# Four graph layers on one core: layer 0 in pairs of seven block products, one tile for the buffers, the softmax division on ScalarE

## Chip, core and metric

One core of a Trainium2 chip runs the whole program. Its engines are TensorE (PE in the profile, with weight loads as PEld), VectorE (DVE), ScalarE (ACT) and GpSimd (POOL); SyncE (SP) issues most of the DMAs. The metric is device time in microseconds, as the median of several runs. One run is also taken with a profile; its own time is given beside its span.

## What is computed

The input x is 128 batches of 128 nodes with 512 features, all fp32. Four graph layers follow one another, each added to its input and normalised over the features:

```python
x = _layernorm(x + _L0_gnn_ref(x, adj, L0_gnn_weight, L0_gnn_bias), axis=-1)
x = _layernorm(x + _L1_gnn_ref(x, L1_gnn_W, L1_gnn_a, L1_gnn_beta, adj), axis=-1)
x = _layernorm(x + _L2_gnn_ref(x, adj, adj, L2_gnn_b), axis=-1)
x = _layernorm(x + _L3_gnn_ref(x, L3_gnn_w_qkv, ..., L3_gnn_ln_beta, adj), axis=-1)
```

The two places that the change concerns are layer 0 and the softmax of layer 3:

```python
# layer 0
y = jnp.einsum('nm,bmd->bnd', adj, x)
out = jnp.einsum('bnd,do->bno', y, weight) + bias
# layer 3, 8 heads of 64
attn = jnp.where(attn_mask[None, None] == 0, -jnp.inf, attn)
attn = jax.nn.softmax(attn, axis=-1)
o = jnp.einsum('bhnm,bhmd->bhnd', attn, v)...
o = o @ w_proj + b_proj
```

Layer 1 is an attention with scores from two vectors per node, layer 2 a maximum over a product with adj. The batches do not depend on each other.

## The kernel before

**Planner.** The kernel is written as chains of steps, one per batch or group of batches (`batch`, L1031, is the main one). Each step asks the class `Plan` (L79) for an engine with an estimate of its work and, if need be, for buffers. `Plan.run` (L172) always takes the step that can start first (ties by urgency, then by the rank of its batch) and issues its instructions at once. So the order on each engine is fixed when the program is built; on the chip each engine runs its list in order and waits by semaphores. Estimates, hand-over times (`HANDOFF`), slack factors (`SLACK`), the margin that PE steps are put back by (`MARGIN`), and the limits per kind of buffer (`CAPS`) decide the order.

**Buffers.** `BUFS` (L49) gives 8 PSUM banks ("ps") and, in SBUF, 21 buffers of 2 KB a partition ("t"), 15 of 4 KB ("q") and 7 of 1 KB ("u"), each a tile of its own. `POOL` tells which kind a use ("x", "yT", "v", "qk", ...) is served from. Ten early batches of x are guests, two by two, in "q" buffers (`GUESTS`, `ROOMS`).

**Groups.** Batches go in groups of four (the last two groups have two). A batch passes layers 0, 1 and 2 by itself or in a pair; the queries, keys and values of layer 3 are made for a group. Weighted values are computed together with the scores of a group six later (`APART`, `tiled`), and by themselves in the last groups.

**Seven block products.** A product of a stacked pair of batches with a 512x512 weight is split into 2x2 blocks, and seven block products with sums of blocks take the place of eight (`seven`, L755). GpSimd makes four differences of the left blocks (`differences`, L833); the weights' sums are made once (`sums`, L547). A block product in `pair_product` (L845) is two matmuls 256 wide. Three banks hold partial sums. Where a partial sum is wanted twice, ScalarE copies it to the output buffer (`kept`, L760) and PE goes on adding to the same bank after that copy; VectorE adds another bank to the copy (`added`, L773). Layer 1 (`layer1`), the queries, keys and values (`section`) and the projection (`projection`) are done so.

**Layer 0.** The first twelve batches (`DIRECT`) take a direct way. From batch 12 on, `mixed_rows` (L337) multiplies by adj (L341), transposes on VectorE in 32x32 squares, and sends the result through DRAM to get it turned (yT). Then PE does one product of four matmuls, 512 wide, with the weight (L1050, by `product`, L314); GpSimd has meanwhile added the bias to x (L307); VectorE adds the product to x with the row sums (L1059), and `layernorm_sums` (L289) normalises, its squares going to the same PSUM bank, which nobody reads.

**Softmax of layer 3.** VectorE adds the mask and takes the negative maximum; ScalarE does one exp per head with the row sums (L1172); VectorE takes reciprocals and multiplies all heads by them in one instruction (L1179), then transposes (L1183). The last two batches (`WHOLE`) do the subtraction, one exp and the sums over all heads at once (L1162 to L1168). After the spill of x to DRAM (all but the last `KEPT` batches) and the fetch back, `normed` (L1291) ends the batch.

Of the kernel before, what the change touches and what calls it, by code (L numbers as in the profile page):

```python
# [15 lines left out]
P = 128  # L16
D = 512
# [5 lines left out]
SOON = (0, 0, 4, 8, 12, 16)  # L23
WHOLE = 2
KEPT = 5
ATTENDS = 2
RUN = 6
# [4 lines left out]
ROOMS = ["v"] * 4 + ["xT"] * 2 + ["qk"] * 5  # L32
STICK = 0.8
CLOSE = 2900
SOFT = 10
PROJ = 0
# [12 lines left out]
BUFS = {"ps": 8, "t": 21, "q": 15, "u": 7}  # L49
POOL = {"x": "t", "xr": "t", "yT": "t", "v": "q", "qk": "q", "xT": "q"}  # L50
CAPS = {"x": 8, "xr": 2, "yT": 6, "v": 4, "qk": 8, "xT": 4}
LAST, AHEAD = 16, 4
DIRECT = 12
LATER = 2
# [8 lines left out]
BORDERS = 0.0  # L63
MARGIN = 0.6
# [14 lines left out]
class Plan:  # L79
# [9 lines left out]
    def __init__(self):  # L89
        self.free, self.requests = {}, []  # L90
        self.slots = {name: [0.0] * n for name, n in BUFS.items()}
        self.caps, self.held = {name: [0.0] * n for name, n in CAPS.items()}, {}
        self.now, self.kind = 0.0, ""
# [21 lines left out]

    def give(self, slot):
        name, i = slot
        self.slots[POOL.get(name, name)][i] = self.now
        if name in CAPS:
            self.caps[name][self.held.pop(slot)] = self.now  # L120
# [16 lines left out]
    def at(self, r):  # L137
        engine, _, take, _, order, _ = r["want"]
        spare = MARGIN if r["ready"] < CLOSE else 0.7
        early = min(spare, r["ready"] / 20) if engine == "PE" and order else 0.0  # L140
        t = max(r["ready"] + early, self.free.get(engine, 0.0))
        names = take()
        for name, i in self.pick(names):
            t = max(t, self.slots[POOL.get(name, name)][i])
        for name in set(names) & set(CAPS):
            t = max(t, sorted(self.caps[name])[names.count(name) - 1])
        return t

    def pick(self, names):

        picked, taken = [], set()
        for name in names:
            pool = POOL.get(name, name)
            free = self.slots[pool]
            i = min((i for i in range(len(free)) if (pool, i) not in taken), key=free.__getitem__)
            picked.append((name, i))
            taken.add((pool, i))
        return picked

    def claim(self, names):  # L160

        got = self.pick(names)
        for name, i in got:
            self.slots[POOL.get(name, name)][i] = float("inf")
            if name in CAPS:
                caps = self.caps[name]
                n = caps.index(min(caps))
                caps[n] = float("inf")
                self.held[name, i] = n
        return got  # L170

    def run(self):  # L172
        while self.requests:
            t, _, _, n = min(
                (self.at(r) + self.border(r["want"]), r["want"][4], r["rank"], n)
                for n, r in enumerate(self.requests)
            )
            assert t < float("inf"), "the chains wait for each other"
            r = self.requests.pop(n)
            t = self.at(r)  # L180
            engine, work, take, late, _, kind = r["want"]
            if engine == "PE":
                work += BORDERS * (kind != self.kind)
                self.kind = kind
            self.free[engine] = t + work
            self.now = r["ready"] = t + work + late
            got = self.claim(take())
            self.step(r, got[0] if len(got) == 1 else got)
# [9 lines left out]
def gnn_stack_kernel(  # L198
# [25 lines left out]

    plan = Plan()
    use, give, done = plan.use, plan.give, plan.done

    def buf(slot, *shape):
        name, i = slot
        return work.tile([P, *shape], F32, name="{}_{}".format(POOL.get(name, name), i))  # L230
# [53 lines left out]
    def row_sums():  # L284

        n = small.tile([P, 6], F32, name="sums", bufs=14)
        return [n[:, c : c + 1] for c in range(6)]

    def layernorm_sums(xb, total, unread):  # L289

        total, nm, squares, ve, rstd, nmr = total
        yield use("DVE", 0.07, follow=True)
        nc.vector.tensor_scalar(nm, total, -1.0 / D, None, op0=ALU.mult)  # L293
        yield use("ACT", 1.03)
        nc.scalar.activation(buf_or_bank(unread), xb, AF.Square, bias=nm, accum_out=squares)  # L295
        give(unread)
        nc.scalar.activation(ve, squares, AF.Identity, bias=eps, scale=1.0 / D)  # L297
        yield from root(ve, rstd)
        yield use("ACT", 1.03)
        nc.scalar.activation(nmr, nm, AF.Identity, scale=rstd)  # L300
        nc.scalar.activation(xb, xb, AF.Identity, bias=nmr, scale=rstd)  # L301
# [99 lines left out]
    wsum_sb = const.tile([P, 3 + SEVEN1 + SEVENP, 3, 2, D // 2], F32, name="wsum_sb")  # L401
# [12 lines left out]
    w0_chunk = [Event() for _ in range(K)]  # L414
    scalars_in, w0_in, w3_in, wa_ready, w3_ready = (Event() for _ in range(5))
# [8 lines left out]
    def load(i, engine="SP", queue=nc.sync):  # L424
        n = i - CAPS["x"]
        if 0 <= n < GUESTS:
            slot = yield use(engine, 0.5, () if n % 2 else ROOMS[n // 2])
            x_slot[i] = x_slot[i - 1] if n % 2 else slot
            if not n % 2:
                room[slot] = buf(slot, 2, D)  # L430
                guests[slot] = 2
            xs[i] = room[x_slot[i]][:, n % 2]
        else:
            x_slot[i] = yield use(engine, 0.5, "x")
            xs[i] = buf(x_slot[i], D)
        queue.dma_start(xs[i], x[i])
        landing(loaded[i], P)

    guests, room = {}, {}

    def leave(i):
        slot = x_slot[i]
        if slot in guests:
            guests[slot] -= 1
            if guests[slot]:
                return
            del guests[slot]
        give(slot)
# [4 lines left out]
    def loads():  # L453
# [30 lines left out]
        landing(w0_in, K * P)  # L484
        yield use("SP", 1.0)
# [52 lines left out]
    def weight(s, name):  # L538

        half, q = D // 2, s * D if s < 3 else 0  # L540
        if name in (S1, S2, S4):
            return wsum_sb[:, s if s < 4 else 3 + SEVEN1, (S1, S2, S4).index(name)]
        k, o = {A11: (0, 0), A12: (2, 0), S3: (0, half), A22: (2, half)}[name]
        w = (wqkv_sb, wqkv_sb, wqkv_sb, w1_sb, wproj_sb)[s]
        return w[:, k : k + 2, q + o : q + o + half]
# [10 lines left out]
    def weight_sums():  # L556

        yield w3_in
        yield use("POOL", 5.8)
        nc.gpsimd.tensor_scalar(  # L560
            wqkv_sb[:, :, :D], wqkv_sb[:, :, :D], HD**-0.5, None, op0=ALU.mult
        )
        for s in range(3):
            yield from sums(s)
        done(w3_ready)
        if SEVENP:
            yield from sums(4)
        done(wproj_ready)

# [31 lines left out]
    class Group:  # L601


        def __init__(self, first, size):
# [13 lines left out]
            self.y, self.y_slot, self.mixed, self.turned, self.h = {}, {}, {}, {}, {}  # L618
            self.begun = [Event() for _ in range(3)]
# [135 lines left out]
    def seven(rank, bx, wide, time, multiply, parts, finished, have, home, housed, slow=0.0):  # L755
# [3 lines left out]

        def kept(p, i, j, event):  # L760
            got = yield use("ACT", copy, lambda: home(j), urgent=True)
# [11 lines left out]
        def added(p, kept, i, j, event):  # L773
            yield kept
            yield use("DVE", sum_, urgent=True)
            for a, c in parts(p, i, j):
                nc.vector.tensor_tensor(c, a, c, op=ALU.add)  # L777
# [41 lines left out]
        def last(bx):  # L819
            yield use("ACT", copy, urgent=True)  # L820
            for a, c in parts(x, 0, 1):
                nc.scalar.copy(c, a)  # L822
# [22 lines left out]
    def pair_product(rank, s, ready, blocks, release, out, finished, differed=None):  # L845
# [29 lines left out]
        def housed(j, slot):  # L875
# [4 lines left out]
            rank, bx, D // 2, 0.87, multiply, parts, finished, have, home, housed,  # L880
# [150 lines left out]
    def batch(i):  # L1031
# [16 lines left out]
        yield w0_chunk[1] if direct else w0_in  # L1048
        bp = yield use("PE", 3.44, "ps")
        p = product(bp, lambda k: yT[:, k, :], lambda k: w0_nat[k] if direct else w0_sb[:, k, :])  # L1050
        w0_left[0] -= direct
        if direct and not w0_left[0]:
            for slot in w0_slot:
                give(slot)
        give(by)
        yield biased
        yield use("DVE", 0.6, urgent=True)
        total = row_sums()
        nc.vector.scalar_tensor_tensor(  # L1059
            xb, p, 1.0, xb, op0=ALU.mult, op1=ALU.add, accum_out=total[0]  # L1060
        )
        yield from layernorm_sums(xb, total, bp)
# [62 lines left out]
        yield use("ACT", 0.61)  # L1125
        nc.scalar.activation(xb, xb, AF.Identity, bias=mx)
        yield from layernorm_dve(xb)
# [48 lines left out]
        yield use("DVE", 1.55)  # L1176
        rs = small.tile([P, H], F32, name="rs3")
        nc.vector.reciprocal(rs, sums)
        nc.vector.tensor_tensor(pr, pr, rs[:, :, None].to_broadcast([P, H, P]), op=ALU.mult)  # L1179
# [48 lines left out]
        else:  # L1228
            yield from (last if i == NB - 1 else usual)(
                i, oT, v, lambda: gr.read(("v", b // 2), 2), fetched  # L1230
            )

# [180 lines left out]
```

## Time and profile before

| | |
|---|---|
| median of 3 runs | 3035.23 us (3034.07 to 3036.01) |
| the profiled execution | 3033.43 us, its span 3031.6 us |
| mean granted TensorE clock | 0.996 |
| DMA | 431.66 MB, mean 142 GB/s |

Layer by layer there is no stage in time: all layers of different batches run at once, and only the start (about 200 us) and the end (about 100 us) differ. In the views of the profile, an L with a number is a line of the kernel; a group's row gives busy time and the mean length of one instruction, and after the next bar the time for which the engine was idle just before, with what ended most of it. Busy times of an instruction and of its readout (ACTIVATION_READ_ACCUMULATOR) overlap on ScalarE, so the step from one start to the next says more than the length.

### The profile page before, as it was taken

What the parts mean: (1) busy time and instruction counts of PE and PEld (TensorE: products, weight loads), DVE (VectorE), ACT (ScalarE), POOL (GpSimd) and SP (SyncE); (2) the same over time, 40 slices, a digit from 0 to 9 for tenths busy, and PEclk for the clock granted to TensorE, in tenths of its full rate; (3) what the DMA queues carried; (4) which work ended last, traced back from release to release, by engine and by line L of the source; (5) the groups of instructions that cost most, each with busy time, mean ns of one, the idle gap of its engine ahead of it and who ended that gap; (6) DMA issues with size and microseconds to landing.
All of it is one profiled execution on the core that took longest, in us unless ns stands there. A gap on an engine that the chain in (4) does not pass through costs nothing. (4 is left out here: it accounts for less than half of the span.)

```text
span 3031.6 us, 51607 instructions
## 1 busy us (share of the span) xinstructions
PE 2986.9 (99%) x15807; PEld 2345.5 (77%) x15807; DVE 2628.8 (87%) x5749; ACT 1938.6 (64%) x5862; POOL 1762.0 (58%) x1814
## 2 busy tenths in 40 slices
PE   9899999999999999999999999999999999999997
PEld 5578787777877778777777777877787777777885
DVE  7999788888888889888888889897898898988878
ACT  4666565666665666666666676566666666756655
POOL 6744655565555656556656556554665545666354
PEclk9999999999999999999999999999999999999999
DMA  5444655456455464646355555554555454554434
GB/s 205 112 124 126 162 141 142 131 150 168 110 142 162 122 168 119 172 130 175 111 148 140 158 153 146 146 141 127 152 160 148 122 145 144 146 154 121 138 90 147
DMA packets 884660, 431.66 MB, mean 142 GB/s; under 512 B 572192, under 2 KB 785824, under 8 KB 884384
## 3 DMA queue, kind: packets, MB, share of 16 engines
q1 hardware_dynamic: 865952, 394.80, 48.2%
q10 hardware_dynamic: 18432, 33.56, 3.0%
q8 instruction: 127, 2.08, 0.3%
q14 instruction: 149, 1.22, 0.1%
HBM read 222.89 MB, written 205.32 MB: 141 GB/s over the span
## 5 line engine op out<-in xcount | busy, mean ns | idle before, releaser
L265 POOL TENSOR_TENSOR sums<-sums,neghalf 128x1 f32<-128x1 f32 x383 | 262.3, 686 | 427.9 <-ACT sums L297 419.9
L314 PE MATMUL ps<-w_sb,t 128*128 128x512 f32 x928 | 417.2, 593 | 2.4 <-DMA t<-x_d 2.1
L1172 ACT ACTIVATE q<-q,nmx 128x128 f32<-128x128 f32 x1008 | 394.2, 395 | 24.6 <-DVE nmx L1158 23.7
L904 PE MATMUL ps<-q,wqkv_sb 128*128 128x256 f32 (+1 forms) x1584 | 359.3, 373 | 0.0
L904 PE MATMUL ps<-q,wsum_sb 128*128 128x256 f32 (+1 forms) x1584 | 357.7, 373 | 0.6 <-POOL q L842 0.5
L904 PEld LDWEIGHTS ps<-q,wqkv_sb 128*128 128x128 f32 x1584 | 293.3, 190 | 56.3 <-issue 16.4
L904 PEld LDWEIGHTS ps<-q,wsum_sb 128*128 128x128 f32 x1584 | 293.2, 190 | 54.4 <-issue 14.0
L265 POOL TENSOR_TENSOR n<-n,neghalf 128x1 f32<-128x1 f32 x257 | 181.2, 706 | 241.0 <-DVE n L260 218.6
L314 PEld LDWEIGHTS ps<-w_sb,t 128*128 128x128 f32 x928 | 175.1, 190 | 181.4 <-issue 172.0
L301 ACT ACTIVATE t<-t,sums 128x512 f32<-128x512 f32 x363 | 295.4, 814 | 12.1
L842 POOL TENSOR_TENSOR q<-q 128x256 f32<-128x256 f32 (+1 forms) x252 | 233.8, 932 | 117.9 <-PE ps L904 66.3
L777 DVE TENSOR_TENSOR q<-ps,q 128x256 f32<-128x256 f32 (+1 forms) x483 | 208.9, 465 | 72.1 <-PE ps L904 54.1
L765 ACT COPY q<-ps 128x256 f32<-128x256 f32 (+1 forms) x483 | 178.5, 410 | 118.1 <-PE ps L904 109.1
L295 ACT ACTIVATE t<-t,sums 128x512 f32<-128x512 f32 x245 | 175.7, 717 | 113.3 <-DVE sums L293 105.2
L765 ACT COPY t<-ps 128x256 f32<-128x256 f32 x378 | 138.5, 367 | 161.6 <-PE ps L855 143.3
L1067 DVE SCALAR_TENSOR_TENSOR t<-t,wa_rows 128x512 f32<-128x512 f32 x236 | 211.8, 899 | 16.6 <-ACT t L301 8.6
L307 POOL TENSOR_TENSOR t<-t,bproj_sb 128x512 f32<-128x512 f32 x124 | 182.2, 1480 | 72.1 <-ACT t L822 66.0
L307 POOL TENSOR_TENSOR t<-t,beta_sb 128x512 f32<-128x512 f32 x118 | 164.0, 1395 | 100.8 <-DVE t L1133 87.7
L855 PE MATMUL ps<-wsum_sb,t 128*128 128x256 f32 x768 | 198.3, 382 | 10.8 <-ACT t L765 9.2
L307 POOL TENSOR_TENSOR t<-t,t 128x512 f32<-128x512 f32 (+1 forms) x126 | 171.6, 1364 | 51.1 <-DMA t<-x_s 43.1
L777 DVE TENSOR_TENSOR t<-ps,t 128x256 f32<-128x256 f32 x378 | 154.2, 415 | 51.9 <-PE ps L855 26.2
L855 PE MATMUL ps<-w_sb,t 128*128 128x256 f32 x768 | 195.7, 379 | 1.9 <-ACT t L333 1.9
(164 smaller groups left out, 7355.6 us busy)
## 6 DMA issues: line engine op xcount, KB each, us to landing
p_d<-t SPq DMA_DIRECT2D x256, 256.0 KB
q<-p_d SPq DMA_DIRECT2D x128, 512.0 KB
x_d<-t SPq DMA_DIRECT2D x244, 256.0 KB
q<-x_d SPq DMA_DIRECT2D x512, 64.0 KB
out<-t ACTq DMA_DIRECT2D x127, 256.0 KB
t<-x_s SPq DMA_DIRECT2D x123, 256.0 KB
t<-in_x SPq DMA_DIRECT2D x117, 256.0 KB
t<-x_d SPq DMA_DIRECT2D x464, 64.0 KB
```

The source lines that it names most:

```text
L265: nc.gpsimd.tensor_tensor(rstd, ve, neghalf, op=ALU.pow)
L295: nc.scalar.activation(buf_or_bank(unread), xb, AF.Square, bias=nm, accum_out=squares)
L301: nc.scalar.activation(xb, xb, AF.Identity, bias=nmr, scale=rstd)
L307: nc.gpsimd.tensor_tensor(dst, dst, other, op=ALU.add)
L314: nc.tensor.matmul(p, lhs(k), rhs(k), start=(k == 0), stop=(k == K - 1))
L765: nc.scalar.copy(c, a)
L777: nc.vector.tensor_tensor(c, a, c, op=ALU.add)
L842: nc.gpsimd.tensor_tensor(blocks(out), blocks(a), blocks(b), op=ALU.subtract)
L855: nc.tensor.matmul(p, t[:, k], w[:, k, :], start=first and k == 0, stop=final and k == 1, skip_group_check=True,)
L904: nc.tensor.matmul(to, lhs, rhs, start=first and j == 0 and k == 0, stop=final and k == 1, skip_group_check=True,)
L1067: nc.vector.scalar_tensor_tensor(unread, xb, 1.0, wa_rows[:, j, :], op0=ALU.mult, op1=ALU.mult, accum_out=gr.s[:, b, j : j + 1],)
L1172: nc.scalar.activation(pr[:, j, :], pr[:, j, :], AF.Exp, bias=nmx[:, j : j + 1], accum_out=sums[:, j : j + 1],)
```

## The change

Four things are changed together.

1. Layer 0 from batch 12 on is done in pairs: `batch` hands yT to a new chain `layer0` per pair, which calls `pair_product` with weight 5. With the new argument `into`, `seven` makes no copies: VectorE adds each partial sum to x itself, at `kept` and `added` and at the last block, and the last addition into each quarter also gives its row sums (two per row, which `layernorm_sums` adds). The squares of the norm go to an SBUF buffer "t" there. The sums of the weight's blocks are made on GpSimd (`layer0_sums`).
2. All work buffers lie in one tile of 105 units of 1 KB a partition. Each use has a size of 1, 2 or 4 units; the planner hands out aligned blocks, and prefers one whose neighbours are taken. Guests are gone.
3. The division of the softmax is done by ScalarE, one instruction a head with the reciprocal as scale, in place of VectorE's single one. The last two batches now do the softmax by heads too (`WHOLE` 0).
4. Constants of the planner: priorities (`SOON`, `PROJ`, `AHEAD`, `LATER`), `KEPT` 5 to 7, `RUN` 6 to 8, `STICK`, `BORDERS`, `MARGIN` and `CAPS`.

```diff
-SOON = (0, 0, 4, 8, 12, 16)
-WHOLE = 2
-KEPT = 5
+SOON = (0, 0, -2, 8, 12, 18)
+WHOLE = 0
+KEPT = 7
-RUN = 6
+RUN = 8
+SEVEN0 = 1
+SUMS2 = 0
+SCALED = 8
-ROOMS = ["v"] * 4 + ["xT"] * 2 + ["qk"] * 5
-STICK = 0.8
+STICK = 0.4
-PROJ = 0
+PROJ = -6
-BUFS = {"ps": 8, "t": 21, "q": 15, "u": 7}
-POOL = {"x": "t", "xr": "t", "yT": "t", "v": "q", "qk": "q", "xT": "q"}
-CAPS = {"x": 8, "xr": 2, "yT": 6, "v": 4, "qk": 8, "xT": 4}
-LAST, AHEAD = 16, 4
+UNITS = 105
+UNIT = 256
+CAPS = {"x": 9, "xr": 2, "yT": 8, "v": 4, "qk": 10, "xT": 4}
+SIZES = {"u": 1, "t": 2, "x": 2, "early": 2, "xr": 2, "yT": 2, "v": 4, "qk": 4, "xT": 4}
+LAST, AHEAD = 16, 6
-LATER = 2
+LATER = 3
-BORDERS = 0.0
-MARGIN = 0.6
+BORDERS = 0.1
+MARGIN = 0.7
...
+    arena = work.tile([P, UNITS * UNIT], F32, name="arena")
...
     def buf(slot, *shape):
         name, i = slot
-        return work.tile([P, *shape], F32, name="{}_{}".format(POOL.get(name, name), i))
+        size = 1
+        for n in shape:
+            size *= n
+        part = arena[:, i * UNIT : i * UNIT + size]
...
+        if unread or pieces == 1:
+            nc.vector.tensor_scalar(nm, total, -1.0 / D, None, op0=ALU.mult)
+        else:
+            nc.vector.tensor_scalar(nm, total, more, -1.0 / D, op0=ALU.add, op1=ALU.mult)
+        got = yield use("ACT", 1.03, lambda: () if unread else ("t",))
...
+        def total(a, c, i, j):
+            if into:
+                nc.vector.scalar_tensor_tensor(
+                    c, a, 1.0, c, op0=ALU.mult, op1=ALU.add, accum_out=into[j][i]
+                )
+            else:
+                nc.vector.tensor_tensor(c, a, c, op=ALU.add)
+
         def kept(p, i, j, event):
+            if into:
+                yield use("DVE", sum_, urgent=True)
+                for a, c in parts(p, i, j):
+                    nc.vector.tensor_tensor(c, a, c, op=ALU.add)
+                done(event)
+                return
...
         def last(bx):
-            yield use("ACT", copy, urgent=True)
+            if into:
+                yield use("DVE", sum_, urgent=True)
+            else:
+                yield use("ACT", copy, urgent=True)
             for a, c in parts(x, 0, 1):
-                nc.scalar.copy(c, a)
+                if into:
+                    total(a, c, 0, 1)
+                else:
+                    nc.scalar.copy(c, a)
...
+        if SEVEN0 and not direct:
+            j = b % 2
+            if h not in gr.y0:
+                gr.y0[h], gr.mixed0[h], gr.added0[h] = {}, Event(2), [Event(2) for _ in range(2)]
+                gr.biased[h], gr.total[h] = {}, {}
+                plan.start(layer0(gr, h, i), i)
+            gr.y0[h][j], gr.y0[h]["slot", j] = yT.rearrange("p (c k) n -> p c k n", c=2), by
+            total = row_sums()
+            gr.biased[h][j], gr.total[h][j] = biased, (total[0], total[6])
+            gr.y0[h]["x", j] = xb
+            done(gr.mixed0[h])
+            yield gr.added0[h][j]
+            yield from layernorm_sums(xb, total, None)
...
-        yield use("DVE", 1.55)
+        yield use("DVE", 0.1 if SCALED == H else 0.1 + 1.45 * (1 - SCALED / H))
         rs = small.tile([P, H], F32, name="rs3")
         nc.vector.reciprocal(rs, sums)
-        nc.vector.tensor_tensor(pr, pr, rs[:, :, None].to_broadcast([P, H, P]), op=ALU.mult)
...
+        for j in range(SCALED):
+            yield use("ACT", 0.2)
+            nc.scalar.activation(pr[:, j, :], pr[:, j, :], AF.Identity, scale=rs[:, j : j + 1])
...
+    def layer0(gr, h, i):
+        yield gr.mixed0[h]
+        y = gr.y0[h]
+        yield gr.biased[h][0]
+        yield gr.biased[h][1]
+        yield w0_ready
+        slot = yield use("POOL", 0.0, "u")
+        t3 = buf(slot, 2, P)
...
+        yield from pair_product(
+            i, 5, gr.mixed0[h], lambda t: t3 if t == T3 else y[t // 2][:, t % 2], release,
+            {j: y["x", j] for j in range(2)}, lambda j: done(gr.added0[h][j]),
+            into=gr.total[h],
+        )
```

## The prediction

> **What bounds the kernel now.** I read the busy shares first, then the same shares by stretch of time, then the chain of waits, then the groups of the lines touched.
>
> ```profile
> span 3031.6 us, 51607 instructions
> PE 2986.9 (99%) x15807; PEld 2345.5 (77%) x15807; DVE 2628.8 (87%) x5749; ACT 1938.6 (64%) x5862; POOL 1762.0 (58%) x1814
> ```
> TensorE (PE) is busy for all but 44.7 us of the span. VectorE (DVE) is next, with 13% to spare.
>
> ```profile
> 60.00:100.00 40.00, 32.53 (x135) 23.27 (x134) 36.25 (x70) 20.27 (x55) 33.92 (x32) 0.91 0.18 44
> 100.00:200.00 100.00, 96.26 (x386) 67.24 (x385) 98.10 (x236) 66.39 (x165) 66.47 (x69) 1.00 0.55 141
> ...
> 1200.00:1600.00 400.00, 400.00 (x2063) 312.75 (x2062) 353.08 (x778) 259.98 (x782) 235.99 (x243) 1.00 0.53 146
> ```
> Columns: stretch, length, busy us of PE, weight loads, DVE, ScalarE (ACT), GpSimd (POOL), granted clock, DMA share, GB/s. From 200 to 2800 us PE is idle for 12.2 of 2600 us at full clock; the first 200 us lose 15.0, all after 2800 us another 17.5. Only up to 200 us does DVE fill its time (98%). So a microsecond less of PE work in the middle is a microsecond less of time, as long as nothing makes PE wait. The chain of waits says the same, and gives pure lengths:
>
> ```profile
> 2205.16 14.01 PE ps L855 x64
> 2223.49 3.43 PE ps L314 x8
> ...
> 2496.22 3.46 PE ps L855 x16
> ```
> Columns: start, length, engine, tile, line, records. Each fp32 matmul leaves two records. A layer 0 product (L314, four 512-wide matmuls) is 8 records in 3.43 us, 0.429 each. Block products of the kind that layer 0 is to get (L855, two 256-wide matmuls, 4 records) run 16 records in 3.46 us, 0.216 each, 0.864 a block product. All records at such paces come to about 2968 us of PE work, so 63 us of the span are start, end and waits.
>
> **PE: the saving.** 116 of the 128 batches (all but the first 12) lose their L314 product: 116 x 3.43 = 397.9 us. 58 pairs get seven block products: 58 x 7 x 0.864 = 350.8. **-47.1 us**, all in the stretch where PE sets the end.
>
> Two rules speak against it. The Trainium skill ("Perfetto Trace Analysis", section Identifying the Most-Contended Engine) says that matmul busy time misjudges TensorE and that the weight-load share should be read; by that, 77% would leave headroom and PE's 99% would prove little. The same page (section Matmuls) prefers larger matmuls. The rows: the 58 x 28 - 116 x 8 = 696 added weight loads at 190 ns are 132 us, which would turn the sum into a loss if they lay open; but in the 0.216 us of a 256-wide record a 0.190 us load fits, and the 3.46 us row has 16 of each. Per column the smaller matmul costs 0.844 against 0.838 ns, and the saving above already has that.
>
> **DVE.** The rows for all three helpers' engines:
>
> ```profile
> L1059 DVE SCALAR_TENSOR_TENSOR t<-ps,t 128x512 f32<-128x512 f32 x118 | 80.6, 683 | 45.7 <-PE ps L314 35.1 <-POOL t L307 5.7 <-DMA q<-x_d 2.7
> L1059 DVE DVE_READ_ACCUMULATOR t<-ps,t 128x1 f32 x118 | 9.6, 82 | 0.0
> L777 DVE TENSOR_TENSOR t<-ps,t 128x256 f32<-128x256 f32 x378 | 154.2, 415 | 51.9 <-PE ps L855 26.2 <-ACT t L765 18.1 <-ACT q L822 2.3
> L1179 DVE TENSOR_TENSOR q<-q,rs 128x1024 f32<-128x1024 f32 x128 | 188.6, 1473 | 4.4
> L842 POOL TENSOR_TENSOR t<-t 128x256 f32<-128x256 f32 x128 | 109.6, 857 | 32.9 <-PE ps L855 28.6 <-POOL t L842 1.1 <-issue 1.1
> L855 PE MATMUL ps<-wsum_sb,t 128*128 128x256 f32 x768 | 198.3, 382 | 10.8 <-ACT t L765 9.2 <-POOL t L842 1.7
> ```
> Busy us and mean ns of one stand behind the bar, then the idle time before and who ended it. Because the partial products are added straight into x, no ScalarE copy is made in layer 0: DVE reads PSUM seven times a pair. Three plain adds at L777's 0.415 = 1.245 us; four that also give row sums, which no row shows at 256 wide: at least 0.415, at most L1059 with its readout, 0.765; I take the nearer end plus the readout, 0.415 + 0.08 = 0.495, so 1.98. Together 3.225 x 58 = 187 us (168 to 250). Removed: L1059 with readout, 116 x 0.765 = 88.7; the division L1179, 188.6; the whole-row softmax of the last two batches (L1162, L1168), 4.8. Net **-95 us** (-114 to -32): DVE goes from 2629 to about 2534, 85% of the new time. Nothing of this sets the end; the work that hides it is PE's own.
>
> **ACT.** 128 x 8 divisions of 128x128 with a scale from a tile. No such row exists. The nearest is L710, also 128 wide with one operand per row:
>
> ```profile
> 1508.20 0.39 ACT L710 ACTIVATE u<-u,logits 128x128 f32<-128x128 f32 x1
> 1508.49 0.19 ACT L710 ACTIVATION_READ_ACCUMULATOR u<-u,logits 128x1 f32 x1
> 1508.59 0.39 ACT L710 ACTIVATE u<-u,logits 128x128 f32<-128x128 f32 x1
> ```
> The next instruction starts 0.29 us after it. At most its whole 0.39; at least about 0.26, the step between 256-wide copies (two of L765 in 0.63, one is 0.37). I take 0.29: 297 us (266 to 404). With some 4 us for the sixteen exps that take the place of L1166 and 3 us for squares that go to SBUF (717 ns) in place of PSUM (688), ACT reaches about 2243 us, **75%**. On the path at 0: a batch's weighted values are wanted only by a later group, and PE has other groups' work meanwhile. But the planner charges 0.2 x 1.1 = 0.22 where I expect 0.29, so ACT falls 0.6 us behind its plan in each batch. Queued behind the eight are the urgent copies L765 and L822 that free PSUM for PE; if that cover goes, the second rival below prices it.
>
> **POOL.** Four differences a pair at the mean of the three L842 groups of layer 1, 0.877 us (109.6, 59.0 and 55.8 us in 256): 58 x 4 x 0.877 = 203 us, and four weight sums for the new matrix, about 6. POOL 1762 to 1971, 66%. Queued behind them are the roots L265 of the layer norms and the adds L307; ScalarE's scaling waits for those, and layer 2's matmul L1118 waits for that, 3.4 us in all today. Cover as for ACT.
>
> **The waits added.** Inside a pair, PE's second, fifth and sixth block products in a bank now wait until DVE, not ACT, has read it. Queued behind that matmul is everything on PE. The like exists: layer 1 and the projection make 126 such products, and PE's waits at L855 are 13.9 us in all (9.2 ACT copies, 1.9, 1.7, 0.9, and 0.2 for the one DVE wait that already is there). From 200 us to 2800 they are only 5.0, about 0.044 a pair: 58 x 0.044 = 2.6 us; with the start's, 58 x 0.11 = 6.4. I take **+2.6**.
>
> **Start.** Up to 200 us some ten batches pass L341, the first step of the batches from 12 on: five pairs with 3.225 - 1.53 = 1.7 us more DVE work each, 8.5 us on a full DVE, before the division's relief comes. PE lost only 3.7 us there at 98% DVE, so most is covered: 0 to 8.5, I take **+1**.
>
> **Edits at nothing.** One tile for all buffers: 105 units of 1 KB instead of 109, and the limits per kind grow (x 8 to 9, yT 6 to 8, qk 8 to 10). PE's 12.2 us in the middle is all that better room can return. KEPT 7 saves two stores and two loads of 256 KB of 431 MB and as many issues on SP. Constants of priority, margin and the wait of a batch for an earlier group (RUN) move instructions on all queues, SP's and POOL's too, without adding any. The end (17.5 us lost) can change by some 4 us either way: DVE loses 1.23 us a batch there, ACT gains 2.3.
>
> **The sum.** The profiled execution took 3033.4 us, 1.8 beyond its span; the median of the runs is 3035.2, 1.8 above that. From the median: 3035.2 - 47.1 + 2.6 + 1.0 = **2992 us** (1.4% faster). Its own range, from the ends above (waits to 6.4, start 0 to 8.5, end 4 either way): 2984 to 3007.
>
> **Rivals.**
> *Less is lost as well (0.10).* Freer buffers and a freer DVE take away the 12.2 us in the middle and 4 at the end: 2976. For it: DVE gets 95 us back. Against it: the waits there are scattered, none over 1.5 us.
> *ScalarE runs late (0.18).* Plan and chip drift by 0.6 us a batch; if PE pays a third, 128 x 0.19 = 24 us: 3016, still faster. For it: ACT has waited for PE so far (L765, 252 us idle before its copies), and that cushion shrinks. Against it: at 75% there is time to catch up.
> *PE stands behind DVE: slower (0.09).* Three of each pair's seven products wait for an in-order engine that is 85% busy, with ops up to 1.2 us (L1158) ahead. It decides from 47.1 / (58 x 3) = 0.27 us a wait on; at 0.4 us, a third of such an op, it is 70 us: 3062. For it: ACT, which they wait for now, is only 64% busy. Against it: the existing DVE wait costs 0.2 us in 126 products, and the order is laid out with a margin.
> *The single tile chains buffers together (0.03).* If the order of accesses were kept per tile and not per range, PE and DVE would take turns, 2921 + 2534, some 5450 us. Against it: ten batches already share double-size buffers in pairs (their load is a q tile) without a wait of that kind.
>
> **Chances.** Likeliest 0.60. About 0.2% either way, some 6 us, is what this kernel's measurement can tell from nothing. Faster: 0.60 + 0.10 + most of the 0.18 = 0.86; within: 0.03 from the tail of the late ScalarE; slower 0.11. The range 2975 to 3018 takes in the better case and the late ScalarE and leaves out the last two and some tails, under 0.2.
>
> **What would show it.** Right: L314 down to some 120 records and the block-product line up by 1624; PE busy some 2940 us and still 98 to 99%; ACT near 75%, with divisions at 0.26 to 0.39; DVE under 2600; waits of PE for DVE at the block products under 10 us. Wrong: PE under 97% in the middle, with its waits ending on DVE adds (third rival) or ACT copies (second); DVE adds with sums near 0.76; a first 200 us that got longer by over 8 us; or a range of PE waits with no producer that fits, which would be the single tile.

## The result and the profile after

The changed kernel takes **3005.28 us** (median of 4 runs, 3004.67 to 3009.23) against 3034.65 before: a ratio of 0.9907, 95% interval 0.9889 to 0.9924, so 23 to 34 us less. The forecast was 2992 with a range of 2975 to 3018. The direction held and the time lies in the range, but of 43 us only 29 came.

The profiled execution is the slowest of the four (3009.23 us). The head of its page, and then its shares by stretch (stretch, length, busy us of PE, weight loads, VectorE, ScalarE and GpSimd, clock, DMA share, GB/s):

```profile
span 3007.5 us, 54842 instructions
PE 2950.5 (98%) x16503; PEld 2476.7 (82%) x16503; DVE 2554.8 (85%) x6023; ACT 2209.8 (73%) x6916; POOL 1886.0 (63%) x2050
```
```profile
60.00:100.00 40.00, 30.37 (x130) 21.82 (x130) 39.19 (x82) 20.75 (x56) 35.68 (x32) 0.95 0.46 109
100.00:200.00 100.00, 96.11 (x428) 77.01 (x429) 95.81 (x244) 64.75 (x159) 74.27 (x81) 0.97 0.36 93
1200.00:1600.00 400.00, 398.39 (x2212) 339.23 (x2211) 350.90 (x835) 301.84 (x956) 260.89 (x280) 1.00 0.54 148
```
PE's records grew by 696, as the replaced products ask for. But PE is idle for 57.1 us of a shorter span, against 44.7 before. Split: 18.2 us in the first 200 us (15.0 before), **23.0 us from 200 to 2800 (12.2 before)**, 15.9 at the end (17.5). PE's busy time fell by 36.4 us, not by 47.1. Part of the other 11 us is short waits that count as busy: with the helpers' work left out ("All three together" below) PE is busy for 2933.7 us with the same 16503 records, 16.8 less. Part is the granted clock (0.995 here, 0.996 before, 0.997 there); a thousandth of it is an estimated 3 us.

The groups that answer to the lines of before, in the same columns:

```profile
L914 PE MATMUL ps<-wsum_sb,arena 128*128 128x256 f32 x2208 | 553.5, 383 | 17.8 <-POOL arena L901 7.8 <-ACT arena L818 6.8 <-DVE arena L811 2.9
L801 DVE SCALAR_TENSOR_TENSOR arena<-ps,arena 128x256 f32<-128x256 f32 x232 | 95.0, 412 | 16.5 <-PE ps L914 15.4
L801 DVE DVE_READ_ACCUMULATOR arena<-ps,arena 128x1 f32 x232 | 18.8, 81 | 0.0
L811 DVE TENSOR_TENSOR arena<-ps,arena 128x256 f32<-128x256 f32 x174 | 71.5, 412 | 12.5 <-PE ps L914 12.0
L1267 ACT ACTIVATE arena<-arena,rs 128x128 f32<-128x128 f32 x1024 | 373.7, 398 | 11.5 <-DVE rs L1259 7.1 <-DVE logits L754 2.2 <-ACT arena L818 0.6
```
In the new kernel's line numbers L914 is the block product of a pair, L963 that of a section, L801 and L811 are the additions into x with and without row sums, L818 ScalarE's copy of a partial sum in all other products, L901 GpSimd's differences, L1267 the division; L346 is ScalarE's scaling in a layer norm, L389 VectorE's transposes in layer 0, L754 a reciprocal of layer 1, L1193 layer 2's product with adj, L386 the product with adj in layer 0 and L1061 the weighted values. The lengths of the single instructions were right: 0.412 + 0.081 us for an addition with sums (0.495 taken), 0.412 for a plain one, and for the division 0.398 us of length; six in a row fill 1.86 us, a step of (1.86 - 0.40) / 5 = 0.29, as taken.

What PE waits for, between 200 and 2800 us (waiter, what ended the wait; us in total, times, longest):

```profile
PE ps L914 <- ACT arena L818: 5.9, 6, 2.2
PE ps L1193 <- ACT arena L346: 3.7, 4, 1.5
PE ps L1193 <- DVE arena L801: 2.6, 2, 1.6
PE ps L963 <- ACT arena L818: 2.0, 4, 1.0
PE ps L914 <- DVE arena L389: 1.8, 1, 1.8
PE ps L914 <- POOL arena L901: 1.5, 3, 0.8
```
No single wait stands out. They are short, and end on ScalarE, VectorE and GpSimd alike; for ScalarE's copies before L855 it was 2.4 us in the same stretch. Which of the new work is behind them the page cannot say. So the experiments leave out one piece of work at a time while the order of all steps stays exactly the same.

### The profile page after: what moved, and what is told of

The parts are those of the page before. It is cut to its first block, busy times and chain, and to the rows that moved or that the text cites. A ratio compares the mean times of both kernels' runs of the same rounds, so it can differ in the third digit from the quotient of the medians.

```text
span 3007.5 us, 54842 instructions
## 1 busy us (share of the span) xinstructions
PE 2950.5 (98%) x16503; PEld 2476.7 (82%) x16503; DVE 2554.8 (85%) x6023; ACT 2209.8 (73%) x6916; POOL 1886.0 (63%) x2050
## 5 line engine op out<-in xcount | busy, mean ns | idle before, releaser
L901 POOL TENSOR_TENSOR arena<-arena 128x256 f32<-128x256 f32 (+1 forms) x868 | 764.8, 890 | 300.3 <-PE ps L914 93.0
L914 PE MATMUL ps<-wsum_sb,arena 128*128 128x256 f32 x2208 | 553.5, 383 | 17.8 <-POOL arena L901 7.8
L914 PEld LDWEIGHTS ps<-wsum_sb,arena 128*128 128x128 f32 x2208 | 414.7, 191 | 105.9 <-issue 17.6
L914 PE MATMUL ps<-w_sb,arena 128*128 128x256 f32 x1952 | 489.7, 379 | 4.7 <-DVE arena L805 2.8
L963 PE MATMUL ps<-arena,wqkv_sb 128*128 128x256 f32 (+1 forms) x2112 | 481.4, 373 | 0.7 <-DVE arena L801 0.7
L963 PEld LDWEIGHTS ps<-arena,wqkv_sb 128*128 128x128 f32 x2112 | 392.4, 190 | 64.1 <-issue 10.0
L818 ACT COPY arena<-ps 128x256 f32<-128x256 f32 (+1 forms) x861 | 311.6, 388 | 166.8 <-PE ps L963 95.7
L914 PEld LDWEIGHTS ps<-w_sb,arena 128*128 128x128 f32 x1952 | 369.4, 190 | 76.2 <-issue 17.5
L1253 ACT ACTIVATE arena<-arena,nmx 128x128 f32<-128x128 f32 x1024 | 404.8, 399 | 16.1 <-DVE nmx L1239 15.7
L1267 ACT ACTIVATE arena<-arena,rs 128x128 f32<-128x128 f32 x1024 | 373.7, 398 | 11.5 <-DVE rs L1259 7.1
L340 ACT ACTIVATE arena<-arena,sums 128x512 f32<-128x512 f32 x371 | 266.1, 717 | 156.4 <-DVE sums L335 96.2
L963 PE MATMUL ps<-arena,wsum_sb 128*128 128x256 f32 (+1 forms) x1584 | 359.4, 373 | 1.9 <-ACT arena L818 1.7
L963 PEld LDWEIGHTS ps<-arena,wsum_sb 128*128 128x128 f32 x1584 | 293.9, 190 | 50.6 <-issue 7.7
L346 ACT ACTIVATE arena<-arena,sums 128x512 f32<-128x512 f32 x383 | 311.6, 814 | 12.8
L1142 DVE SCALAR_TENSOR_TENSOR arena<-arena,wa_rows 128x512 f32<-128x512 f32 x256 | 260.1, 1018 | 21.4 <-ACT arena L346 16.4
L914 PE MATMUL ps<-wproj_sb,arena 128*128 128x256 f32 x992 | 244.7, 382 | 0.3 <-DVE arena L1231 0.3
L963 PE MATMUL ps<-wqkv_sb,arena 128*128 128x256 f32 x1024 | 243.4, 380 | 0.0
L963 PEld LDWEIGHTS ps<-wqkv_sb,arena 128*128 128x128 f32 x1024 | 194.5, 191 | 38.7 <-issue 10.1
```

Of the source, the lines that this page charges most:

```text
L901: nc.gpsimd.tensor_tensor(blocks(out), blocks(a), blocks(b), op=ALU.subtract)
L914: nc.tensor.matmul(p, t[:, k], w[:, k, :], start=first and k == 0, stop=final and k == 1, skip_group_check=True,)
L963: nc.tensor.matmul(to, lhs, rhs, start=first and j == 0 and k == 0, stop=final and k == 1, skip_group_check=True,)
L1142: nc.vector.scalar_tensor_tensor(unread, xb, 1.0, wa_rows[:, j, :], op0=ALU.mult, op1=ALU.mult, accum_out=gr.s[:, b, j : j + 1],)
L1253: nc.scalar.activation(pr[:, j, :], pr[:, j, :], AF.Exp, bias=nmx[:, j : j + 1], accum_out=sums[:, j : j + 1],)
L1267: nc.scalar.activation(pr[:, j, :], pr[:, j, :], AF.Identity, scale=rs[:, j : j + 1])
```

## Experiments

In what follows A, B and C are the theories named in the first expectations: ScalarE late, gaps in the order, PE behind VectorE. Times are medians; the kernel before, run beside them, had 3034.0 to 3035.4 us.

### Work left out under an unchanged order

**The division on ScalarE.** Chip: 2987.04 us (ratio 0.984, 0.9826 to 0.9855), **18.2 us** below the changed kernel.

```diff
         for j in range(SCALED):
             yield use("ACT", 0.2)
-            nc.scalar.activation(pr[:, j, :], pr[:, j, :], AF.Identity, scale=rs[:, j : j + 1])
```

> The changed kernel with the 1024 divisions on ScalarE left out and everything else, the order of the steps on every engine too, as it is (the softmax stays undivided). It prices the division alone. Theory A (ScalarE runs late: the division at 0.29 us a head against 0.22 in the plan delays the copies that PE waits for): most of the 23 us that PE loses more than before between 200 and 2800 us come back, 2980 to 2990 us. Theory B (the order has the gaps: PE has no other step ready between the dependent steps of a product): 0 to 5 us, 3000 to 3005 us, though ScalarE loses some 300 us of work. Theory C (PE waits for VectorE's additions into x): as B.

The waits of PE between 200 and 2800 us in this kernel:

```profile
PE ps L1193 <- DVE logits L754: 2.2, 1, 2.2
PE ps L914 <- DVE arena L389: 1.8, 1, 1.8
PE ps L1193 <- ACT arena L346: 1.6, 3, 0.8
PE ps L963 <- ACT arena L818: 1.0, 1, 1.0
PE ps L1193 <- DVE arena L801: 1.0, 1, 1.0
...
PE ps L914 <- ACT arena L818: 0.7, 1, 0.7
```
The waits for copies L818 went from 7.9 (5.9 and 2.0) to 1.7 us, those of layer 2's matmul for the scaling L346 from 3.7 to 1.6. This is what A asked for, and B's 0 to 5 us is refuted. A's reason, a plan that charges too little, is not shown by it: leaving the division out takes away both the lag and the work. But it does not yet say that ScalarE is the worse place for the division.

**The division on VectorE, in the kernel before.** Chip: 3022.66 us beside 3034.01 (ratio 0.996, 0.9946 to 0.9975), **11.4 us** less.

```diff
         nc.vector.reciprocal(rs, sums)
-        nc.vector.tensor_tensor(pr, pr, rs[:, :, None].to_broadcast([P, H, P]), op=ALU.mult)
```

> The kernel before with its 128 divisions on VectorE left out and the order of all steps kept (the softmax stays undivided). It is the counterpart of leaving out the division on ScalarE, which brought 18 us in the changed kernel. Theory A (the division on ScalarE is what delays PE; on VectorE it was covered): 0 to 5 us faster than before, 3030 to 3035 us. Rival (either engine's division delays PE about as much, so moving it neither cost nor gained): 12 to 20 us faster, 3015 to 3023 us.

11.4 us lies just under the rival's 12. The division had cost some 11 us where it was. Moving it cost 18.2 - 11.4 = 6.8 us net. By the ratios' intervals the 18.2 is uncertain by an estimated 7 us either way and the 11.4 by 4, so the sign of the net is likely but not shown.

**Three of seven additions of a pair.** Chip: 2995.01 us (0.9868, 0.9851 to 0.9884), **10.3 us** below the changed kernel.

```diff
             if into:
                 yield use("DVE", sum_, urgent=True)
-                for a, c in parts(p, i, j):
-                    nc.vector.tensor_tensor(c, a, c, op=ALU.add)
                 done(event)
```

> The changed kernel with three of the seven additions of a layer 0 pair left out: those of the partial sums that PE goes on adding to (174 additions of 256 columns; layer 0 is then incomplete). The order is the same; PE's second, fifth and sixth product in that bank need not wait for VectorE. Theory C (these waits took the gain): 15 us or more come back, under 2990 us. Theory A: 0 to 3 us. Theory B: the gaps of the order shrink where they are such waits, above all in the first 800 us: 3 to 10 us, 2995 to 3002 us.

That is less than C's 15, at the top of what B had. An addition left out brings 10.3 / 174 = 0.059 us, and this holds both PE's wait for it and the 0.41 us that it takes of VectorE. It is far from the 0.27 from which the change would have been lost, but it is not the 2.6 us in all that the prediction took.

**Three of four differences of a pair.** Chip: 2998.55 us (0.988, 0.9865 to 0.9894), **6.7 us** below; the interval overlaps that of the changed kernel, so this price is not clear of the noise. It lies between the two theories' bounds.

```diff
-            nc.gpsimd.tensor_tensor(blocks(out), blocks(a), blocks(b), op=ALU.subtract)
+            if out == T3 or not left_out:
+                nc.gpsimd.tensor_tensor(blocks(out), blocks(a), blocks(b), op=ALU.subtract)
```
Here `left_out` is true for layer 0 alone.

> The changed kernel with three of the four GpSimd differences of a layer 0 pair left out (T1, T2 and T4; 174 instructions of some 0.88 us; the products then take blocks that are not differences). Same order. Theory A (ScalarE) and C (VectorE): 0 to 3 us faster than the changed kernel. Rival, that GpSimd's new work delays the roots and PE: 8 us or more, below 2997 us.

**All three together.** Chip: 2975.55 us (0.9807, 0.9794 to 0.982), 29.7 us below the changed kernel; the sum of the three alone is 35.2.

> The changed kernel with the division, the three additions and the three differences of a pair all left out, in the same order. Alone they brought 18, 10 and 7 us. If the three delays are different waits of PE: near their sum, 2968 to 2976 us. If they are the same waits, each shortened by any of the three: little beyond the largest, 2982 to 2987 us.

Mostly different waits, then, as far as prices with intervals of several us can say. The same stretch of this kernel and of the kernel before without its division, first the one, then the other:

```profile
200.00:2800.00 2600.00, 2592.47 (x14605) 2211.62 (x14604) 2182.74 (x5154) 1723.82 (x5238) 1503.26 (x1626) 1.00 0.54 146
```
```profile
200.00:2800.00 2600.00, 2593.63 (x13743) 2048.93 (x13742) 2111.54 (x4884) 1697.44 (x5149) 1442.08 (x1564) 1.00 0.52 143
```
PE idles 7.5 us in the one and 6.4 in the other. And their times differ by 3022.66 - 2975.55 = 47.1 us, which is the PE time that seven products in place of eight save. The two have different orders, so that the numbers meet to a tenth is luck. What speaks for their meeting within a few us is that PE idles about as long in both, over the whole span too: 2974.6 - 2933.7 = 40.9 and 3023.3 - 2984.3 = 39.0 us.

### Parts undone, with a new order

**Layer 0 without pairs.** Chip: 3044.89 us (1.0031, 1.002 to 1.0042), 39.6 us slower than the changed kernel and 10 slower than before, inside the first theory's range; the rival, that the pairs bring nothing, is refuted for these constants. But the order is a new one, and the next two runs show what an order can cost, so the 39.6 us are not the price of the pairs alone.

```diff
-SEVEN0 = 1
+SEVEN0 = 0
```

> The changed kernel with layer 0 as before (one product of four 512-wide matmuls a batch), all else changed; the planner lays out a new order. Theory that the pairs bring their PE time of 47 us less what they lose in waits: some 25 to 45 us slower than the changed kernel, 3030 to 3050 us. Rival, that the pairs bring nothing and the gain is that of the buffers and the division: 3005 us or less.

**The planner's old constants.** Chip: 3097.2 us (1.0204, 1.0186 to 1.0221), **92 us** slower than the changed kernel, with the same matmuls, layer 0 in pairs.

```diff
-SOON = (0, 0, -2, 8, 12, 18)
-WHOLE = 0
-KEPT = 7
-RUN = 8
-STICK = 0.4
-PROJ = -6
-LAST, AHEAD = 16, 6
-LATER = 3
-BORDERS = 0.1
-MARGIN = 0.7
+SOON = (0, 0, 4, 8, 12, 16)
+WHOLE = 2
+KEPT = 5
+RUN = 6
+STICK = 0.8
+PROJ = 0
+LAST, AHEAD = 16, 4
+LATER = 2
+BORDERS = 0.0
+MARGIN = 0.6
...
```
CAPS goes back too.

> The changed kernel with the planner's constants and limits of the kernel before (SOON, WHOLE, KEPT, RUN, STICK, PROJ, AHEAD, LATER, BORDERS, MARGIN, CAPS); pairs, one tile and ScalarE's division stay. If the constants only move steps (as the prediction put them at nothing): 2995 to 3015 us. Theory B (the layout decides how much of the PE time saved is seen): tens of us slower, 3035 to 3080 us, with the same PE work and longer waits.

Its page and its stretches:

```profile
PE 2977.1 (96%) x16503; PEld 2489.1 (80%) x16503; DVE 2575.1 (83%) x6027; ACT 2206.6 (71%) x6886; POOL 1902.0 (61%) x2050
```
```profile
400.00:800.00 400.00, 385.05 (x2122) 324.54 (x2121) 331.54 (x792) 288.09 (x895) 241.20 (x268) 0.98 0.50 135
1600.00:2000.00 400.00, 387.17 (x2125) 324.07 (x2124) 345.34 (x803) 297.30 (x935) 251.68 (x272) 1.00 0.52 142
2800.00:3101.00 301.00, 253.43 (x1586) 211.82 (x1584) 198.50 (x431) 192.39 (x629) 135.21 (x151) 0.92 0.37 108
```
and, over the whole span, what PE waited for:

```profile
PE ps L914 <- POOL arena L901: 17.8, 14, 3.6
PE ps L1061 <- DMA arena<-p_d: 16.9, 2, 16.4
PE ps L963 <- DMA arena<-x_d: 13.0, 1, 13.0
PE ps L386 <- DMA arena<-in_x: 12.4, 2, 11.6
PE ps L914 <- ACT arena L818: 10.6, 9, 2.8
```
That is beyond even theory B's 3080. PE and GpSimd have exactly the records of the changed kernel, VectorE and ScalarE within 30. PE stands because the next step in its order has no data yet: before loads (L386, 12.4 us; L963, 13.0 us at once), before weighted values at the end (L1061, 16.4 us at once). It is idle for 124 us of the span of 3100.9, 67 more than in the changed kernel. The other 27 us are in its busy time (2977.1 against 2950.5), and the granted clock goes with them: 0.984 in the mean against 0.995, and 0.92 in the last 301 us, where PE idles for some 47. The difference in the clock is worth an estimated 0.011 x 3100.9 = 34 us, some of it while PE idled.

**The buffers in one tile, alone.** The kernel before but for the tile and its handing out by size: 3064.81 us (1.0099, 1.0083 to 1.0114), 30.2 us slower than before, at the edge of the first theory's 30.

```diff
-SEVEN0 = 1
+SEVEN0 = 0
-SCALED = 8
+SCALED = 0
...
```
and the constants and CAPS as in the kernel before, 105 units.

> One part of the change alone: buffers in one tile of 105 units handed out by size, with layer 0, the division and all constants as before. If the tile only changes which buffer a step gets, and so the order: within 30 us of before, PE's work and weight loads unchanged, no waits of a new kind. If accesses were ordered by tile: hundreds of us slower. If the free handing out by size is itself a gain: 5 to 15 us faster than before.

What PE waited for from 2900 us on:

```profile
PE ps L1061 <- DMA arena<-p_d: 24.8, 2, 19.3
PE ps L914 <- ACT arena L818: 1.8, 2, 1.2
PE ps L914 <- POOL arena L901: 1.5, 1, 1.5
```
From 200 to 2800 us PE idles 13.0 us, as before (12.2). The tile does not chain the buffers together: the prediction's fourth rival is refuted. It changes which step gets a buffer first, and this order leaves PE two waits, 24.8 us together, for the turned softmax at the end; in all PE idles 70.5 us against 44.7. Being free to hand out by size was no gain by itself.

**The division back on VectorE.** 3019.28 us (0.9951, 0.9934 to 0.9967), 14 us slower than the changed kernel: the rival's side of the expectation. VectorE is busy for 2725 us, 90% of the span.

```diff
-SCALED = 8
+SCALED = 0
```

> The changed kernel with the division back on VectorE for all heads (SCALED 0), pairs, one tile and constants kept; the planner lays out a new order. Theory A (ScalarE's load costs 18 us and VectorE would cover it): 2985 to 3000 us. Rival (VectorE, with layer 0's additions and the division, is as late as ScalarE was): 3003 to 3020 us.

**The division charged as it is.** 3019.1 us (0.9949, 0.9934 to 0.9963), 13.8 us slower.

```diff
+DIVC = 0.264
...
-            yield use("ACT", 0.2)
+            yield use("ACT", DIVC)
```

> The changed kernel with the division charged at 0.264 x 1.1 = 0.29 us a head in the plan, as measured, in place of 0.22; nothing else is changed, the order is new. Theory A in its strict form (the chip falls behind a plan that charges too little): PE's waits for ScalarE's copies shrink and some 10 us come back, 2990 to 3000 us. Theory B (what the layout happens to be decides): anywhere within 20 us of the changed kernel, slower as likely as faster, while PE waits for copies less.

PE's waits between 200 and 2800 us (lines one later than in the changed kernel):

```profile
PE ps L1194 <- ACT arena L347: 6.3, 6, 2.2
PE ps L368 <- DMA arena<-e_d: 5.7, 3, 3.7
PE ps L964 <- ACT arena L819: 3.4, 4, 1.5
PE ps L915 <- DVE arena L812: 2.8, 5, 1.0
```
The waits of the pairs for copies (5.9 us before) are gone from that list, as A's strict form asked; the sections' waits for copies (L964, 2.0 us before) rose to 3.4. PE now waits for layer 1's weights (L368), the layer norm and the additions. The time rose. This is theory B: here a more truthful plan was not a better order.

### A tried improvement: the division split between the engines

Six or four heads on ScalarE, the rest in one VectorE instruction, order unchanged: 3013.11 us (0.9931, 0.9918 to 0.9943) and 3015.33 us (0.9937, 0.9924 to 0.9949). By medians 8 and 10 us slower than the changed kernel; by ratios to the kernel before, the first interval overlaps that of the changed kernel and the second meets it at its edge. Both are slower than every range that was expected.

```diff
+        nc.vector.tensor_tensor(
+            pr[:, 6:], pr[:, 6:], rs[:, 6:, None].to_broadcast([P, 2, P]), op=ALU.mult
+        )
         for j in range(SCALED):
             yield use("ACT", 0.2)
-            nc.scalar.activation(pr[:, j, :], pr[:, j, :], AF.Identity, scale=rs[:, j : j + 1])
+            if j < 6:
+                nc.scalar.activation(pr[:, j, :], pr[:, j, :], AF.Identity, scale=rs[:, j : j + 1])
```

> The changed kernel, complete and in the same order, with six heads divided on ScalarE and the last two by one VectorE instruction right after the reciprocal. ScalarE's six take 6 x 0.29 = 1.74 us, what the plan charges for eight (1.76); VectorE gets some 0.35 us a batch that the plan does not know. If ScalarE's lag behind the plan is what the division costs: 5 to 12 us faster than the changed kernel, 2993 to 3000 us. If any work on either engine delays PE alike: within 3 us of it, 3002 to 3008 us.

> As the split after six heads, with four heads on each engine: ScalarE 1.16 us a batch, VectorE some 0.65. Lag theory: no further gain over six, since ScalarE is then ahead of its plan, and a loss from VectorE: 2995 to 3005 us. Load theory (each microsecond of ScalarE's division delays PE in proportion, 18 us for all of it, VectorE's 12 us): about 9 back and 6 lost, 3000 to 3004 us.

ScalarE kept to the planned sum and nothing came back, so the lag theory finds no support. It is not cleanly refuted, since VectorE got more work than was meant. Its instruction (L1265), in the kernel with six:

```profile
L1265 DVE TENSOR_TENSOR arena<-arena,rs x128: 424/426/1536, 230.5 to 2969.4; 128x256 f32<-128x256 f32 x128
```
Minimum, median and maximum in ns: 0.43 us when alone, up to 1.54 us; the mean is 0.62, not the 0.35 of the expectation. The likely reading, not shown by a run of its own, is that 79 us more of VectorE's time outweighed 256 divisions less on ScalarE. No complete kernel of this study beats the changed one.

## Why the prediction was right in direction and too large

**What bounds it, and PE's saving: right.** -47.1 us rests on two rows. Under the same constants the pairs are worth 39.6 us net of their waits, with a new order in it, and the two kernels with helper work left out are 47.1 apart. The weight loads stayed hidden; the loads' share rose from 77 to 82% while the time fell, so the rule that looked at that share, set beside the saving in the prediction, had no force here.

**The prices of the new work: right; the totals missed what the work does to its neighbours.** VectorE went to 2555 us (2534 forecast), ScalarE to 2210 (2243), GpSimd to 1886 (1971). GpSimd's 85 us are not a wrong price of the differences. The heads of two pages, the changed kernel with the division back on VectorE and the kernel before without it:

```profile
PE 2951.4 (98%) x16503; PEld 2478.3 (82%) x16503; DVE 2725.0 (90%) x6151; ACT 1934.1 (64%) x5892; POOL 1967.2 (65%) x2050
```
```profile
PE 2984.3 (99%) x15807; PEld 2345.8 (78%) x15807; DVE 2448.9 (81%) x5621; ACT 1942.9 (64%) x5862; POOL 1683.9 (56%) x1814
```
With the division on VectorE GpSimd's busy time is 1967.2 us, close to the forecast, with the same 2050 instructions (in a new order); without it the kernel before has 1683.9 in place of 1762.0, with the same 1814 in the same order. So the division on VectorE had lengthened GpSimd's instructions by some 80 us, and the prediction, which took it off VectorE, left that out of GpSimd's sum. The last section shows the same in the other direction.

**"On the path at 0" and "cover as for ACT": the step that failed.** The prediction took +2.6 us for the added waits (+3.6 with the start), nothing for the moved division and nothing for the differences, because PE has other work meanwhile. Measured under a fixed order: 10.3 us for the additions, 6.7 for the differences, and for the division 18.2 where it is now against 11.4 where it was, net 6.8. Together 23.8; they overlap (29.7 measured for 35.2 summed), so the net shortfall is about 29.7 - 11.4 = 18.3 us. What is missing from 47.1 is 47.1 - 29.4 = 17.7. The balance is an estimate: the 10.3 us are not net of layer 0's old additions (L1059), which no run left out, and the orders differ. The price of the waits was read from what PE waits for today at the like products, 0.044 us a pair (the products that wait are the third, fifth and sixth by the code, not the second; the number of three holds); measured, the additions cost 10.3 / 58 = 0.18 a pair. That row only shows the waits left after the planner has arranged other steps around the products, and says nothing of the next piece of work on a queue that is 58 to 87% full.

**The start and the end: right in size.** PE's idle time in the first 200 us grew by 3.2 (forecast +1, at most 8.5), at the end it fell by 1.6 (4 either way).

**"Edits at nothing": right only as a bundle, for a wrong reason.** It was argued that constants move instructions without adding any and that the tile can return at most 12 us. A new order with nearly the same work is worth 92 us (old constants with the new work) and 30 us (the tile alone). That the bundle came out well is luck as far as the prediction goes: its argument would have said the same of the bundle at 3097.

**The signs.** All that were named for "right" came: 120 records left of L314 (L359 now), 1624 more of the block products, PE busy 2950.5 us at 98%, ScalarE at 73%, divisions 0.29 us apart, VectorE under 2600, PE's waits for VectorE at the block products 7.8 us. They could not tell a gain of 43 us from one of 29, since each looks at one engine's busy time or at the waits that the profile names.

**The rivals.** ScalarE late, with 24 us given back, named the largest single delay (18 us) but not that VectorE's division had cost 11 of them already. PE behind VectorE exists at 0.059 us a wait instead of 0.27 or more. (The waits in the middle before, called none over 1.5 us, have one of 1.7, L855 for L842; it changes nothing.) The better case did not come. The single tile is refuted.

Open: which of the constants carries the 92 us, how much of the 29.4 us is owed to the order of the changed kernel, and whether the net price of moving the division is 6.8 us or nothing; the split runs, in which VectorE took part of it, speak for the move having been no loss in this order, without showing it.

## To carry to other kernels

Where one engine is full and all others run in order beside it, price their work by leaving it out under an unchanged order, not by the waits that the profile shows: 262 us of ScalarE's busy time (2209.8 to 1947.9) that "hid" behind PE cost 18 us here. An edit to a kernel whose order is laid out by a planner is two edits, the work and the new order, and the second was worth up to 92 us here; compare single edits only under a fixed order, or with the constants fitted to each. And a more exact charge in such a planner was one more change of order here, not a correction.

## Not expected of the hardware

In this kernel VectorE's instructions with two tensor operands in SBUF have long tails, those that read one of the two from PSUM have none. Minimum, median and maximum in ns, in the changed kernel:

```profile
L1142 DVE SCALAR_TENSOR_TENSOR arena<-arena,wa_rows x256: 641/884/1770, 26.9 to 2792.4; 128x512 f32<-128x512 f32 x128
L811 DVE TENSOR_TENSOR arena<-ps,arena x174: 363/413/426, 97.4 to 2766.7; 128x256 f32<-128x256 f32 x174
```
and the first of them in the kernel before, under its old line number:

```profile
L1067 DVE SCALAR_TENSOR_TENSOR t<-t,wa_rows x236: 644/692/1767, 26.5 to 2778.3; 128x512 f32<-128x512 f32 x118
```
The instruction is the same. In the kernel before, 20 more read a "q" buffer; with these its 256 took 232.9 us, and they take 260.1 in the changed kernel. The median misleads, because the lengths fall into two heaps, one at 0.69 us and one mostly over 1.0. In the changed kernel's trace, 83 of the 256 ran while no GpSimd addition or difference (256 or 512 columns wide) was running: they took 0.686 us in the mean and never more than 0.693. The other 173, which overlapped one, took 1.177 us in the mean, and all 134 that took over 0.75 us are among them. In the kernel before 82 of 256 took over 0.75 us; the median jumps when that share passes one half. Without 174 of GpSimd's differences the median is back at 693 ns, but the mean only went from 1018 to 985. With the division back on VectorE GpSimd is busiest of all (1967.2 us), and the median is 693 too: what counts is which instructions meet, so how long an engine is busy depends on the order too. The additions into x, with one operand in PSUM, never took more than 0.426 us; the 92 of L811 that overlapped such a GpSimd instruction took 0.411 us in the mean, the others 0.413.

The Trainium skill ("GPSIMD Engine Reference", section 1. Specifications) says that GpSimd shares its SBUF interfaces with VectorE and that instructions with two SBUF inputs contend. The rows agree, and put a price on it: some 0.49 us in the mean for such an instruction that meets a GpSimd one, and 1.1 us at the worst on the split division. VectorE fell by 74 us where 95 were worked out; the 27 us more at this one line are over the 21 that are missing, and other lines moved by less, both ways.
